# Two attention blocks and two feed-forward blocks on one core: the splitting of the score maxima may go to GpSimd, three release times are set anew, and the order is drawn again

## The chip, the cores and the metric

One core of a Trainium2 chip runs the whole program. The engines are TensorE (PE in the profile; its weight loads are PEld), VectorE (DVE), ScalarE (ACT), GpSimd (POOL) and SyncE (SP), which here only issues DMAs. Every engine works through its own list of instructions in a fixed order and waits at the head of it until what the instruction needs is ready. The metric is device time in microseconds. Before the change it was 1161.88 us, the median of 3 runs (1161.06 to 1162.78).

## The reference, cut to what matters

The input is 128 sequences of 64 tokens with 128 features, and a context of the same shape. Four residual blocks follow one another:

```python
x = x + L0_xattn(layernorm(x), ctx)   # 16 heads of 8, layer norms, gate, layer norm of the output
x = x + L0_ffn(layernorm(x))          # silu(w1 x) * (w2 x); two 512x512 layers with gelu; w3
x = x + L1_xattn(layernorm(x), ctx)   # 16 heads of 8, biases
x = x + L1_ffn(layernorm(x))          # relu(W1 x + b1), W2, b2

# inside either attention block
scores = einsum('bhqd,bhkd->bhqk', q, k) * 8 ** -0.5
attn = softmax(scores, axis=-1)
out = einsum('bhqk,bkhd->bqhd', attn, v) @ Wo + bo
```

The softmax subtracts the maximum of each row of scores. In the kernel this maximum is one per query, per group of heads, and it is taken off the scores by a matmul.

## The kernel before, in words

**Tiles.** The 8192 tokens are cut into 16 chunks of 512 tokens, 8 sequences each. For each chunk there are four stages: `attention0`, `ffn0`, `attention1` and `ffn1`. An attention stage has a part for the context (`context0` or `context1`: keys and values) and one for the queries, and then two halves (`attend`) of four sequences each.

**One half of an attention** (lines 614 to 712): 16 score matmuls write four PSUM banks (L629); VectorE takes the negated maxima over the keys out of PSUM, 128x32 numbers (L633, "max"); four small instructions split each of them into three bfloat16 numbers whose sum is the maximum (L642 to L645, "parts"); TensorE transposes these (L649, "max transpose"), ScalarE copies them out (L652), TensorE writes the scores again with the maxima taken off (L661, "scores less max"), ScalarE takes the exponential (L666), TensorE forms the weighted values and their sums (L680), ScalarE and VectorE sort these by masks (L690, L691, L693, L694), VectorE takes the reciprocal and shuffles it (L697, L698), and GpSimd multiplies (L712). Two such halves are followed by the product with the output weights (L740).

**The feed-forward block `ffn0`** has four gated pieces (L872 and L873 on TensorE, L876 on ScalarE, L878 and L879 on VectorE). Its two 512x512 layers are done with seven products of quarter matrices in place of eight (L928); for that GpSimd forms four differences of the activations for each layer (L910), and once, at the start, four sums of the weights for each layer (L865, in `weights`). These sums write tiles `ws` and `wh`. All products of a layer come after its weight sums.

**The order.** No engine's list is written out by hand. A planner in the kernel (`Order`) runs while the program is built. Each stage is a generator that yields operations (`Op`) with an engine or a choice of engines; `LENGTHS` gives the length of each operation on each engine, `RESOURCES` the number of buffers. At each step the planner takes, among all streams that could go on, the operation with the earliest start, and among equals the one with the lowest priority number plus a small random draw. The draws depend on `DRAWS`, one seed for each 50 us of the planner's clock; a seed of 0 means no draw. Where an operation names two engines, the planner takes the one on which it would end first (`start_of`). It also keeps GpSimd operations and those VectorE operations that are named in `PORT` ("z", "parts", "gate sums", "gained") from running at the same time in its plan. Whatever it assumes, on the chip each engine only follows its list and its semaphores.

**What is loaded when.** SyncE issues the loads of the start in one queue: context and tokens of chunk 0, `col`, the head mask, `wa0`, chunk 1, `row` (the vectors that are added along the features, on all partitions), `w12`, `wh` (2 MB), chunk 2, and four further weights. The planner knows of these by a list of made-up loads, `landed`, whose times it takes as given: a stream whose `ends` hold one of them isn't planned before that time. In the kernel before there are six; the weight sums of both layers are released by the last one, at 20.0.

**Two output biases.** `out_bias` (L436 to L444) multiplies the bias of the values by the output weights on TensorE (L440), and adds the output bias from `row` on VectorE (L443). The one for the first attention block is `early_bias`. It has no release time in the kernel before; its addition waits on the chip until `row` has landed.

**Fillers.** While its clock is below 95 (`RAMP`), the planner puts small matmuls on a blank tile (L405) where it expects TensorE to be idle.

Of the kernel before, what the change touches and what calls it, by code (L numbers as in the profile page):

```python
# [11 lines left out]
ALU = mybir.AluOpType  # L12
# [22 lines left out]
for _n, _w in _COLS:  # L35
# [17 lines left out]


STRETCH = 50.0
DRAWS = [121, 0, 0, 0, 0, 384, 0, 0, 0, 615, 0, 0, 0, 0, 0, 0, 0, 67, 0, 0, 564, 0, 762, 0]
SPREAD = 0.1
SWAP = [*range(16, 32), *range(16)]

# [2 lines left out]
PE, DVE, ACT, POOL, SP = "PE", "DVE", "ACT", "POOL", "SP"  # L62
# [9 lines left out]
        "product": (0.865, -0.2), "f1": (0.865, -0.2),  # L72
    },
    DVE: {
        "bias+": 0.28, "masks": 1.2, "gate weights": 0.4, "folds": 1.9, "moments": 1.07, "z": 1.05, "copied": 0.68,
        "scaled": 0.75, "qx": 1.5, "kx": 1.5, "vb": 1.8, "max": 2.3, "parts": 0.8, "reciprocal": 2.2, "o2": 0.83,
        "from bank": 0.68, "gate sums": 1.3, "gate": 0.4, "gained": 1.1, "gated": 1.45, "sum": 0.68, "saved": 0.68,
        "relu": 0.7,
# [3 lines left out]
        "two masked": 0.84, "gate exp": 0.25, "tanh": 0.69, "saved": 0.59, "gelu": 0.91, "relu": 0.69,  # L82
    },
    POOL: {
        "blank": 0.2, "blank values": 2.1, "rsqrt": 1.84, "rsqrt gate": 2.15, "oT": 0.73, "add": 1.27,
        "difference": 1.27, "weights": 1.27,
    },
    SP: {"load": (0.9, 4.0), "load again": (0.9, 4.0), "store": (0.5, 3.0)},
# [63 lines left out]
class Order:  # L152
# [63 lines left out]
    def draw(self):  # L216

        self.drawn += 1
        seed = DRAWS[min(int(self.clock[PE] / STRETCH), len(DRAWS) - 1)]
        x = (self.drawn * 2654435761 + seed * 2246822519) & 0xFFFFFFFF  # L220
# [83 lines left out]
def kernel(  # L304
# [16 lines left out]
    nc = tc.nc  # L321
# [13 lines left out]
    def tile_of(slot, shape, dtype=F32):  # L335

        kind, i = slot
        if kind != "bank":
            return work.tile(list(shape), dtype, tag=f"{kind}{i}", name=f"{kind}{i}")
        n = 1  # L340
        for d in shape[1:]:
            n *= d
        t = banks[:, i, :]
        t = t[:, 0:n] if dtype is F32 else t.bitcast(dtype)[:, 0:n]
        if len(shape) == 2:
            return t
        names = "abc"[: len(shape) - 1]
        return t.rearrange(
            "p (" + " ".join(names) + ") -> p " + " ".join(names), **dict(zip(names[1:], shape[2:]))
        )  # L350
# [49 lines left out]
    blank = const.tile([P, P], BF16, tag="blank", name="blank")  # L400
# [27 lines left out]
    def colv(name, k=0):  # L428
        s = COL[name]
        return col[:, s.start + k : s.start + k + 1]  # L430
# [5 lines left out]
    def out_bias(w, bv, bo, tag):  # L436

        pe = yield Op(PE, "bias", get={"bank": 1})
        ps = tile_of(pe.slots["bank"][0], (P, D))
        nc.tensor.matmul(ps, colv(bv).to_broadcast([P, P]), w, start=True, stop=True)  # L440
        yield Op(DVE, "bias+", put=pe.slots["bank"])
        t = const.tile([P, D], F32, tag=tag, name=tag)
        nc.vector.tensor_tensor(t, ps, row[:, ROW[bo], :], ALU.add)  # L443
        biases[tag] = t.unsqueeze(1).to_broadcast([P, NG, D])  # L444
# [36 lines left out]
    biases, masked, gates, folded, early_bias, late = {}, [], [], [], [], []  # L481
    made_weights, weights_of = {}, []
# [131 lines left out]
    def attend(got, half):  # L614
# [17 lines left out]
        m = small.tile([P, 4, 2 * HS], F32, tag="m", name="m")  # L632
# [4 lines left out]
            ALU.max,  # L637
            negate=True,
        )
        yield Op(DVE, "parts")  # L640
        part = [nm[:, :, 8 * j : 8 * j + 8] for j in range(3)]
        nc.vector.tensor_copy(part[0], m)  # L642
        nc.vector.tensor_tensor(m, m, part[0], ALU.subtract)
        nc.vector.tensor_copy(part[1], m)
        nc.vector.tensor_tensor(part[2], m, part[1], ALU.subtract)  # L645
        yield folded
        pe = yield Op(PE, "max transpose", get={"bank": 1, "nmT": 1}, put=mx.slots["nm"])
        pt = tile_of(pe.slots["bank"][0], (P, P), BF16)
# [1 line left out]
        op = yield Op(ACT, "max copied", put=pe.slots["bank"])  # L650
# [44 lines left out]
        op = yield Op(DVE, "reciprocal", get={"rec": 1}, put=pv.slots["su"])  # L695
# [6 lines left out]
        if "oT" not in got:  # L702
            given = got["oT given"] = Stream(None, 0, ())
            got["oT"] = None
            op = yield Op(POOL, "oT", get={"wk": 1}, put=done)
# [8 lines left out]
    def attention(got, prio):  # L714

        halves = []
        for half in range(2):
            halves.append((yield (attend(got, half), prio)))
        yield halves
        yield Op(NONE, "free", put=got["free"])  # L720
        return got["oT"].rearrange("p h s q -> p (h s q)"), got["oT_slots"]
# [97 lines left out]
    def attention0(ci, prio):  # L819
        got = {"free": []}  # L820
        xt = x_sb[ci]
        con = yield (context0(ci, got, prio), prio)
        if ci < 2:
            yield Op(NONE, "free", after=landed[3 * ci + 1])
        z, fz = yield from normalised(xt, twice=True)
        qnT, fq = yield from transposed(z, (), colv("L0_xattn_ln_q_g"), colv("L0_xattn_ln_q_b"))
        gat = yield (gate0(z, fz, got), prio)
        got["qx"], f = yield from queries(wa0[:, 0, :], qnT, bq0, fq)
        got["free"] += f
        yield [con]  # L830
        add = yield (biased0(xt), prio)
        oT, fo = yield from attention(got, prio)
        po, fp, fw = yield from token_major([(groups(oT), wa0[:, 3, :])], fo, own=True)
        yield early_bias
        yield Op(DVE, "from bank", put=fp)
        o = tile_of(fw[0], (P, NG, D))
        nc.vector.tensor_tensor(o, po, biases["bo0"], ALU.add)
        yield [gat]
        y, fy, rs = yield from normalised(
            o, gate=got["gate"], gain=row[:, ROW["L0_xattn_ln_o_g"], :]  # L840
        )
        yield [add]
        yield Op(DVE, "gained", put=fy + fw)
        for g in range(NG):
            nc.vector.scalar_tensor_tensor(  # L845
                xt[:, g, :], y[:, g, :], rs[:, g : g + 1], xt[:, g, :], ALU.mult, ALU.add
            )
# [4 lines left out]
    def weights(l):  # L852

        a = [[wh[:, l, 2 * j : 2 * j + 2, 256 * i : 256 * i + 256] for j in range(2)] for i in range(2)]
        s = [ws[:, l, n] for n in range(3)]
        for out, x, y, f in (
            (s[0], a[1][0], a[1][1], ALU.add),
            (s[1], s[0], a[0][0], ALU.subtract),  # L860
            (a[1][0], a[0][0], a[1][0], ALU.subtract),
            (s[2], a[0][1], s[1], ALU.subtract),
        ):
            yield Op(POOL, "weights")
            nc.gpsimd.tensor_tensor(out, x, y, f)  # L865

        made_weights[l] = [a[0][0], a[0][1], s[2], a[1][1], s[0], s[1], a[1][0]]
# [119 lines left out]
    def ffn0(ci, prio):  # L987
        xt = x_sb[ci]
        z, fz = yield from normalised(xt)
        zT, fz = yield from transposed(z, fz)  # L990
        fz = Last(fz, 4)
        b, made = {}, []
        yield from two_halves(b)
        for k in range(4):
            made.append((yield (gated(k, zT, fz, b), prio)))
        yield made[:1]
        h = [Both(made[0], made[1]), Both(made[2], made[3])]
        ready = [[h[0], h[0]], [h[1], h[1]]]
        for l in range(2):
            c = {}  # L1000
            ready = yield from square(l, b, ready, c, prio)
            b = c
            if l == 0:
                marks[ci].done = True
        yield ready[0] + ready[1]
        ps, fp, fw = yield from token_major(
            [
                (lambda g, k=k: b[k // 2][0][:, g // 2, k % 2, g % 2 * P : g % 2 * P + P], w3[:, k, :])
                for k in range(4)
            ],  # L1010
            b[0][1] + b[1][1],
            own=True,
        )
        yield Op(DVE, "from bank", put=fp)
        y = tile_of(fw[0], (P, NG, D))
        nc.vector.tensor_tensor(y, ps, rowv("L0_ffn_w3_s"), ALU.mult)
        yield Op(POOL, "add", put=fw)
        nc.gpsimd.tensor_tensor(xt, xt, y, ALU.add)
# [67 lines left out]
    order.add(loads(), 0)  # L1086
    a0, f0, a1, f1 = [], [], [], []

    landed = [Op(SP, "load") for _ in range(6)]
    for op, us in zip(landed, (0.0, 0.8, 2.2, 4.0, 5.0, 20.0)):  # L1090
        op.end, op.lag = us, 0.0
    early_vb, early_nm = order.take("vb", N_VB), order.take("nm", N_NM)
    order.add(blanks(), 1.2)
# [3 lines left out]
    folded.append(order.add(folds(), 1.6))  # L1097
    for l in range(2):
        weights_of.append(order.add(weights(l), 2.5 + l))
        weights_of[l].ends = [landed[5]]  # L1100
    early_bias.append(order.add(out_bias(wa0[:, 3, :], "L0_xattn_bv", "L0_xattn_bo", "bo0"), 1.5))
    for ci in range(NCH):
        marks.append(Stream(None, 0, ()))
        pa = 1 if ci else 0.5
        a0.append(order.add(attention0(ci, pa), pa, a0[-2:-1] + arrived[ci : ci + 1] + marks[-AHEAD - 1 : -AHEAD]))
        if ci == 0:
            late.append(order.add(out_bias(wa1[:, 3, :], "L1_xattn_b_v", "L1_xattn_b_o", "bo1"), 1.5, a0))
        first = ci == NCH - 1
        pf = -0.5 if first else 3 + ci / 100
        f0.append(order.add(ffn0(ci, pf), pf, [a0[ci]] + f0[-2:-1]))  # L1110
        a1.append(order.add(attention1(ci, 0), 0, [f0[ci]] + a1[-2:-1]))
        f1.append(order.add(ffn1(ci, 4), 4, [a1[ci]] + f1[-5:-4]))
# [52 lines left out]
```

## Time and profile before

The profiled execution took 1162.56 us; the span from its first to its last instruction is 1160.7 us, so 1.9 us lie around it. The mean granted TensorE clock was 0.989.

| engine | busy us | share of the span | instructions |
|---|---|---|---|
| PE | 1111.9 | 96% | 13758 |
| PEld | 867.8 | 75% | 13758 |
| DVE | 894.9 | 77% | 2239 |
| ACT | 724.6 | 62% | 1262 |
| POOL | 461.7 | 40% | 685 |

A row of the profile's list of groups names a line, an engine and an operation, what it writes and reads, the number of instructions, and after the bar their busy time and the mean of one. These are the rows that the change bears on:

| line, engine | what | count | busy us | mean ns |
|---|---|---|---|---|
| L633 DVE | maxima | 64 | 146.0 | 2282 |
| L642 DVE | parts, first copy | 64 | 16.6 | 260 |
| L643 DVE | parts, first difference | 64 | 16.6 | 260 |
| L644 DVE | parts, second copy | 64 | 16.0 | 249 |
| L645 DVE | parts, second difference | 64 | 14.3 | 224 |
| L865 POOL | weight sums | 8 | 10.3 | 1264 to 1294 |
| L443 DVE | output biases | 2 | 0.6 | 284 |
| L405 PE | fillers | 248 | 22.4 | 256 (pipelined) |

A wait is put down to what ended last before the waiting instruction could start. TensorE's busy time counts the fillers too, so it isn't all of use.

### The profile page before, as it was taken

How to read it: one execution, taken by the hardware profiler on the slowest of the kernel's cores; microseconds unless marked ns; L12 is line 12 of the kernel's file. 1: busy time of each engine (PE TensorE's matmuls, PEld its weight loads, DVE VectorE, ACT ScalarE, POOL GpSimd, SP SyncE). 2: the span in 40 equal slices, each digit the busy share in tenths (PEclk: the TensorE clock that was granted, in tenths of full speed). 3: DMA queues.
4: the chain of work that ended last, by engine and by line, in shares of the span. 5: the costliest groups of instructions: out<-in, count | busy, mean ns of one | idle time of the engine just before them, and what ended most of it. 6: DMA issues, size and time to landing. Idle time of an engine off the chain costs nothing. (4 is left out here: it accounts for less than half of the span.)

```text
span 1160.7 us, 32599 instructions
## 1 busy us (share of the span) xinstructions
PE 1111.9 (96%) x13758; PEld 867.8 (75%) x13758; DVE 894.9 (77%) x2239; ACT 724.6 (62%) x1262; POOL 461.7 (40%) x685
## 2 busy tenths in 40 slices
PE   7688999999999999999999999999999999999998
PEld 6557777876688767786788768876877788687776
DVE  6787798978768967888898877699587889647671
ACT  4365766676876657657667757575676656645643
POOL 7234343633523525424444325353336433434220
PEclk9799999999999999999999999999999999999999
DMA  7000100010000100000000010100010200000001
GB/s 251 2 11 1 28 2 20 11 29 1 20 11 3 38 11 19 11 29 11 2 2 3 2 37 2 38 2 2 2 37 1 65 2 3 11 10 1 2 30 37
DMA packets 35378, 23.21 MB, mean 20 GB/s; under 512 B 1440, under 2 KB 34208, under 8 KB 35104
## 3 DMA queue, kind: packets, MB, share of 16 engines
q1 hardware_dynamic: 35232, 21.13, 6.1%
q8 instruction: 108, 1.77, 0.6%
q14 instruction: 38, 0.31, 0.1%
HBM read 16.93 MB, written 4.19 MB: 18 GB/s over the span
## 5 line engine op out<-in xcount | busy, mean ns | idle before, releaser
L633 DVE TENSOR_REDUCE m<-banks 128x32 f32<-128x2048 f32 x64 | 146.0, 2282 | 17.9 <-PE banks L629 17.6
L712 POOL TENSOR_TENSOR wk<-av,rec 128x256 f32<-128x256 f32 x64 | 46.8, 731 | 280.8 <-DVE rec L698 207.9
L666 ACT ACTIVATE e<-banks 128x2048 f32<-128x2048 f32 x64 | 120.1, 1877 | 38.3 <-PE banks L661 36.4
L928 PE MATMUL banks<-wk,wh 128*128 128x256 f32 x512 | 127.1, 385 | 0.0
L928 PE MATMUL banks<-hd,wh 128*128 128x256 f32 x512 | 125.8, 384 | 0.8 <-ACT nmT L652 0.8
L928 PE MATMUL banks<-wk,ws 128*128 128x256 f32 x512 | 125.3, 385 | 0.0
L947 ACT ACTIVATE hd<-hd,col 128x256 f32<-128x256 f32 x192 | 85.4, 499 | 42.7 <-DVE hd L954 42.3
L697 DVE RECIPROCAL su<-su 128x256 f32<-128x256 f32 x64 | 111.5, 1742 | 0.0
L928 PEld LDWEIGHTS banks<-wk,ws 128*128 128x128 f32 x512 | 94.9, 192 | 18.4 <-issue 5.0
L928 PEld LDWEIGHTS banks<-hd,wh 128*128 128x128 f32 x512 | 93.2, 190 | 19.2 <-issue 3.8
L928 PEld LDWEIGHTS banks<-wk,wh 128*128 128x128 f32 x512 | 94.8, 191 | 15.3 <-issue 1.0
L954 DVE TENSOR_TENSOR hd<-banks,hd 128x512 f32<-128x512 f32 x96 | 65.2, 686 | 50.9 <-PE banks L928 35.0
L500 POOL TENSOR_TENSOR nr<-nv,neg_half 128x4 f32<-128x4 f32 x96 | 97.5, 1015 | 8.0
L486 ACT COPY hd<-banks 128x512 f32<-128x512 f32 x73 | 42.8, 586 | 85.5 <-PE banks L928 83.8
L910 POOL TENSOR_TENSOR wk<-hd,wk 128x512 f32<-128x512 f32 x64 | 81.7, 1278 | 36.1 <-DVE hd L879 17.5
L539 ACT ACTIVATE wk<-x,nb,nr 128x128 f32<-128x128 f32 x204 | 83.4, 484 | 14.5 <-POOL nb L530 13.5
L629 PEld LDWEIGHTS banks<-kx,qx 32*128 32x128 f32 x2048 | 63.8, 186 | 24.9 <-issue 7.6
L680 PEld LDWEIGHTS banks<-e,vblk 128*32 128x32 f32 x4096 | 60.2, 110 | 28.6 <-ACT e L666 12.1
L629 PE MATMUL banks<-kx,qx 32*128 32x128 f32 x2048 | 75.7, 283 | 5.1 <-DVE m L633 2.0
L680 PE MATMUL banks<-e,vblk 128*32 128x64 f32 x4096 | 70.4, 220 | 4.9 <-ACT e L666 4.7
L661 PE MATMUL banks<-qx,kx 32*128 32x128 f32 x2048 | 74.0, 284 | 0.0
L910 POOL TENSOR_TENSOR wk<-hd 128x512 f32<-128x512 f32 x32 | 40.9, 1279 | 79.9 <-ACT hd L947 36.1
(132 smaller groups left out, 2383.8 us busy)
## 6 DMA issues: line engine op xcount, KB each, us to landing
c<-in_c_dram SPq DMA_DIRECT2D x32, 256.0 KB, 3.1
x<-in_x_dram SPq DMA_DIRECT2D x16, 256.0 KB, 3.4
out_dram<-x SPq DMA_DIRECT2D x16, 256.0 KB, 2.3
wh<-in_w_h_dram SPq DMA_DIRECT2D x1, 2048.0 KB, 13.3
wa<-in_w_a_dram SPq DMA_DIRECT2D x2, 256.0 KB, 5.4
w<-in_w_dram SPq DMA_DIRECT2D x1, 512.0 KB, 7.3
wf<-in_w_f_dram SPq DMA_DIRECT2D x2, 256.0 KB, 7.0
row<-in_rows_dram SPq DMA_DIRECT2D x1, 384.0 KB, 6.6
```

Of the source, the lines that this page charges most:

```text
L500: nc.gpsimd.tensor_tensor(rs, ve, neg_half, ALU.pow)
L539: nc.scalar.activation(z[:, g, :], src[:, g, :], AF.Identity, bias=nb[:, g : g + 1], scale=rs[:, g : g + 1])
L629: nc.tensor.matmul(sc[:, g, s, :], qs[h, s, :], ks[h, s, :], start=True, stop=True)
L633: nc.vector.tensor_reduce(m, sc.rearrange("p g s (j k) -> p g (s j) k", j=2), AX.X, ALU.max, negate=True,)
L661: nc.tensor.matmul(sT[:, g, s, :], lhs, rhs, start=(n == 0 and s == 0), stop=(n == 1), skip_group_check=True)
L666: nc.scalar.activation(e.rearrange("p g s i q -> p (g s i q)"), sT.rearrange("p g s c -> p (g s c)"), AF.Exp, scale=SCALE,)
L680: nc.tensor.matmul(po[32 * g : 32 * g + 32, i, s, :], vb[:, 4 * (half * HS + s) + g, i : i + 2].rearrange("p h j d -> p (h j d)"), e[:, g, ...
L697: nc.vector.reciprocal(su, su)
L910: nc.gpsimd.tensor_tensor(T[n][0], x(), y(), ALU.subtract)
L928: nc.tensor.matmul(pieces[bank][0][:, o], w[:, k, o * P : (o + 1) * P], x[:, k], start=(new and k == 0 and o == 0), stop=(k == 1), skip_gr ...
L947: nc.scalar.activation(out(i, t)[:, o], (src or out(i, t))[:, o], AF.Gelu, scale=colv(scale, 2 * i + o))
L954: nc.vector.tensor_tensor(out(i, t), pieces[bank][0], out(i, t), ALU.add)
```

## The change: what it does

1. "parts" may be on VectorE or on GpSimd, by the planner's choice, half by half. Its length on GpSimd is set to 1.05; on VectorE it stays at 0.8.
2. The length of "z" on VectorE goes from 1.05 to 1.3.
3. The list `landed` has nine times in place of six. The weight sums of layer 0 are released at 24.0 and those of layer 1 at 40.0, in place of 20.0 for both. The first output bias is released at 7.2.
4. `DRAWS` has other seeds, so the planner draws another order.

```diff
-DRAWS = [121, 0, 0, 0, 0, 384, 0, 0, 0, 615, 0, 0, 0, 0, 0, 0, 0, 67, 0, 0, 564, 0, 762, 0]
+DRAWS = [583, 0, 0, 858, 0, 0, 0, 0, 2, 0, 0, 0, 0, 0, 0, 0, 0, 0, 174, 0, 0, 687, 994, 0]
...
-        "bias+": 0.28, "masks": 1.2, "gate weights": 0.4, "folds": 1.9, "moments": 1.07, "z": 1.05, "copied": 0.68,
+        "bias+": 0.28, "masks": 1.2, "gate weights": 0.4, "folds": 1.9, "moments": 1.07, "z": 1.3, "copied": 0.68,
...
-        "blank": 0.2, "blank values": 2.1, "rsqrt": 1.84, "rsqrt gate": 2.15, "oT": 0.73, "add": 1.27,
+        "blank": 0.2, "blank values": 2.1, "parts": 1.05, "rsqrt": 1.84, "rsqrt gate": 2.15, "oT": 0.73, "add": 1.27,
...
-        yield Op(DVE, "parts")
+        op = yield Op((DVE, POOL), "parts")
+        by = nc.gpsimd if op.engine == POOL else nc.vector
         part = [nm[:, :, 8 * j : 8 * j + 8] for j in range(3)]
-        nc.vector.tensor_copy(part[0], m)
-        nc.vector.tensor_tensor(m, m, part[0], ALU.subtract)
-        nc.vector.tensor_copy(part[1], m)
-        nc.vector.tensor_tensor(part[2], m, part[1], ALU.subtract)
+        by.tensor_copy(part[0], m)
+        by.tensor_tensor(m, m, part[0], ALU.subtract)
+        by.tensor_copy(part[1], m)
+        by.tensor_tensor(part[2], m, part[1], ALU.subtract)
...
-    landed = [Op(SP, "load") for _ in range(6)]
-    for op, us in zip(landed, (0.0, 0.8, 2.2, 4.0, 5.0, 20.0)):
+    landed = [Op(SP, "load") for _ in range(9)]
+    for op, us in zip(landed, (0.0, 0.8, 2.2, 4.0, 5.0, 7.2, 12.0, 24.0, 40.0)):
...
-        weights_of[l].ends = [landed[5]]
+        weights_of[l].ends = [landed[7 + l]]
     early_bias.append(order.add(out_bias(wa0[:, 3, :], "L0_xattn_bv", "L0_xattn_bo", "bo0"), 1.5))
+    early_bias[0].ends = [landed[5]]
```

The arithmetic is the same in both kernels. What the built lists show of the new order: of the 64 splittings of maxima 38 are on GpSimd and 26 on VectorE; there are 259 fillers in place of 248; ScalarE loads its tables 69 times in place of 67; some copies and maskings have changed between ScalarE and VectorE. SyncE's first sixteen loads are in the same order as before. At the start VectorE's list now has the moments of chunk 0, the gate weights, the masks, the folds, the moments of chunk 1's context, the scaling of chunk 0's query side, the moments of chunk 1's tokens, and only then the output bias. The list then holds the attention of the chunks 0, 1 and 2 to its end before the first gated piece of `ffn0`, and from there the `ffn0` of the chunks 0 and 1 side by side; in the kernel before the first gated piece of chunk 0 comes before the maxima of chunk 2 are transposed.

## The prediction

> **What bounds the kernel now.** I read the row of slices first, then busy time in three stretches, then what TensorE waits for in the first 100 us, then VectorE's timeline there.
>
> ```profile
> PE   7688999999999999999999999999999999999998
> DVE  6787798978768967888898877699587889647671
> PEclk9799999999999999999999999999999999999999
> ```
>
> Each digit is a fortieth of the span, 29 us. TensorE is full from the fifth slice to the end; only the start has holes. The next view gives busy us of PE, PEld, DVE, ACT and POOL, then granted clock, DMA share and GB/s.
>
> ```profile
> 0.00:50.00 50.00, 33.76 (x551) 29.19 (x551) 32.24 (x107) 20.37 (x38) 27.65 (x49) 0.90 0.45 146
> 50.00:100.00 50.00, 40.23 (x548) 30.32 (x552) 41.69 (x120) 21.92 (x39) 17.87 (x33) 0.90 0.02 7
> 100.00:1160.00 1060.00, 1037.88 (x12675) 808.33 (x12663) 820.94 (x2014) 682.30 (x1185) 416.15 (x603) 1.00 0.05 15
> ```
>
> TensorE idles 16.2 + 9.8 = 26.0 us before 100 us, and 22.1 in the other 1060, some 4 of them at the end. Of its busy time before 100 us some 22 are fillers (L405, no use). So about 48 of the first 100 us are not work; later there are only 18 us to win. Who holds it up at the start, by total wait:
>
> ```profile
> PE banks L649 <- DVE nmax L642: 4.1, 1, 4.1
> PE banks L760 <- DVE gw L757: 4.0, 1, 4.0
> PE banks L553 <- DVE m L633: 3.5, 2, 1.9
> PE banks L740 <- DVE m L633: 3.4, 1, 3.4
> ```
>
> VectorE ends every one of them. Its own timeline (start, duration, then idle before and releaser) shows two faults:
>
> ```profile
> 5.70 0.36 DVE L514 BATCH_NORM_AGGREGATE mv<-st 128x2 f32<-128x6 f32 x4
> 10.99 0.29 DVE L443 TENSOR_TENSOR bo<-banks,row 128x128 f32<-128x128 f32 x1 [4.93 <-DMA row<-in_rows_dram]
> ...
> 27.05 1.35 DVE L805 SCALAR_TENSOR_TENSOR wk<-wk,gw 128x128 f32<-128x128 f32 x1
> ...
> 31.99 0.18 DVE L642 CAST nmax<-m 128x32 bf16<-128x32 f32 x1
> 32.21 1.20 DVE L643 TENSOR_TENSOR m<-m,nmax 128x32 f32<-128x32 f32 x1
> 33.44 0.18 DVE L644 CAST nmax<-m 128x32 bf16<-128x32 f32 x1
> ```
>
> First, the output bias waits 4.93 us for `row`, with masks, gate weights and folds queued behind it. Second, beside GpSimd's back-to-back adds (L865 and L817, 23.1 to 33.4) a gate sum takes 1.35 us where it takes 0.28 later, and L643 1.20 instead of 0.19.
>
> **The bias (part 3) and the order of the start.** I walk the new list with these durations. TensorE: 60 fillers end at 6.9, 19 more at 0.062 (28 took 1.73) at 8.1, the gate product 0.75 at 8.85. VectorE does moments and masks meanwhile, then the gate copy 0.26 and folds 1.84: 10.95. The same block ends at 14.50 before: a lead of 3.5. `row` landed at 10.9 before (issued 4.27, 6.6 to landing), and the bias now comes at about 14, behind moments and scaling, so its wait goes; SP's queue up to `row` is unmoved. What is late next is ScalarE's scaling of the two inputs and TensorE's fixed list: first scores at 17.6 (21.8 before).
>
> The first maximum then starts at 20.45 (one of four gate sums still meets an add), and the second follows at once, ending at 24.9; before, four slowed gate sums lay between and it ended at 31.9. Lead 7.0. Here comes a loss: the second half's splitting is on VectorE, and from 24.0 GpSimd has the first weight sum, an add of chunk 1 and three more sums back to back. If each of the four small instructions meets one, as L643 did, they take 4 times 1.2 and end at 29.4 (lead 5.1 on 34.5); if not, at 25.9. I take the first, by the gate sums, of which three in a row did so. Then scaling 0.8, query product 0.9, the second scores 2.5: first exponential at 34.0 (38.6 before), last reciprocal of chunk 0 at 44.6 (49.2 before): lead 4.6.
>
> From there to the `ffn0` part VectorE has 34.5 us of work by the rows (four maxima 9.1, two reciprocals with shuffles 4.3, five moments of 1.1 to 1.2, the rest small) and waits: for GpSimd's last weight sums at the two "gained" groups, for ScalarE's normalised inputs, for chunk 2's exponentials. I get the first gated piece at 87.5. TensorE has then done 37.6 us of work: three attention chunks of 12.0 (transposes 0.9, k, q and v 2.7, scores 2.1, transposed maxima 0.2, second scores 2.9, weighted values 2.2, output 0.9; chunk 2 without output), biases and two transposes. So 49.9 us are not work. Before, the same sum at 99.6 gives 46.0 of work and 53.6 lost. **Lead 3.7**; without the collision 7.2. After it two `ffn0` run side by side, six gated pieces of 1.73 on TensorE against 1.45 on VectorE, so no new hole is due.
>
> **Weight sums (part 3).** Eight adds of about 1.28, 10.3 us in all, no more and no fewer; L865 started at 23.1 before, so 24.0 moves layer 0 little. Behind them in GpSimd's queue stand chunk 0's products (L712), splittings, and square roots. The products need these weights only near 90 us. Cost: the collisions counted above, nothing else.
>
> **Splitting (part 1).** 38 halves of 64 move. VectorE loses 38 x (260 + 260 + 249 + 224) = 37.7 us; with the copies and maskings moved between it and ScalarE (kx -16, qx +6, copies and scalings +28 instructions) it has about 31 us less, 864 in all; ScalarE has 4 less. GpSimd has no such row. Its nearest are 128x256 at 731, 128x512 at 1278 and 128x4 at about 200: 2.14 ns an element gives 0.25 for 128x32, at least 0.20. Four are 0.8 to 1.0, plus 0.08 between dependent ones (L499 at 5.20 for 0.19, L500 at 5.48) and 0.14 for the handover: I take 1.4, range 1.2 to 1.5, against 0.86 for VectorE's chain undisturbed and 1.1 on average. A half's maxima arrive 0.3 to 0.5 later. After 100 us TensorE's order has other chunks' work between scores and transposed maxima; idle there was 1.9 us in 3 waits for L645. Where that cover is gone, a late half costs its lateness. I take zero for TensorE after 100 us: VectorE's relief and the handover bear on the same 18 us of holes.
>
> **A rule that speaks against it.** The Trainium skill, "Perfetto Trace Analysis", section "Optimizing Scalar/DVE Operations", says that GpSimd and VectorE share an SBUF port, so shifting work between the two may gain nothing. The row shows the lock: L643 has a median of 192 ns, a mean of 260 and a maximum of 1269; means over medians (82, 68, 67, 32 ns) make 15.9 us of lock in 64 halves. By the rule, 38 x 1.0 us of port time only change hands and VectorE gains nothing. By the rows it is freed of 37.7 us, 9.5 of them lock (38/64 of 15.9), and the new GpSimd pieces can hold it 0.25 us each at most, 38 us if all 152 did, which they can't: most of VectorE's time is PSUM maxima, reciprocals and reads of banks. I take the rows. Neither shows on TensorE directly.
>
> **"z" and the draws.** The length changes no instruction; its rows say 4 x 450 ns on VectorE, and the list has four instructions fewer there. Two more table loads are 2.6 us on ScalarE (62% busy), hidden by its idle time. The draws move all the rest. Bound: all 18 us of holes gone, or as many new ones. I take zero. The end of TensorE's list has more than 10 us of other work between the last output product and the last normalised tile, and the closing L1049 and L740 groups as before: zero.
>
> **Sum.** Span 1160.7 - 3.7 = 1157.0; with the 1.9 around it 1158.9; the median of the runs shown lies 0.7 under the profiled 1162.56: **1158 us**.
>
> **Rivals.**
> *The relief also closes holes later.* For it: VectorE ends the most waits of TensorE after 100 us (about 10 of 18 us). Against: such holes come from order as well. Half of 18 closed and the start 2 us better: 1162 - 3.7 - 2 - 5 = 1151.
> *The lead is given back.* In-order lists meet later at the same draining of three chunks; collisions at "gained" cost more than I count. No change: 1162.
> *Slower: GpSimd's queue becomes the late one.* Its place is L642 to L645 behind square roots (L500, 1.02) or differences (L910, 1.28). For it: 38 new entries with a strict order, and a transposed maximum that comes late stops TensorE's whole list. Against: GpSimd is 40% busy (43% after). If 13 of 38 come 1.28 late uncovered, 16.6 us: 1162 - 3.7 + 16.6 = 1175. It decides from four late halves on (5.1 against 3.7).
> *It doesn't do what it says*: ruled out, the built list has 38 on GpSimd.
>
> **Chances.** Forecast 0.46, its own range 1152 to 1163; holes closed 0.14; given back 0.14; slower 0.26. A measurement tells about 0.2%, 2.3 us, from no change: 1159.6 to 1164.2 is "the same". Faster: 0.39 of the forecast and 0.14: 0.53. Same: 0.07, 0.10 of "given back" and 0.02: 0.19. Slower: the rest, 0.28. The range: 1149 (just beyond the second case) to 1170 (half of the slow case's way).
>
> **What would show it.** Right: L443 without a wait for `row`; second maximum ending near 25 us, first gated piece at 85 to 90; fewer than 26 us of TensorE idle before 100; splitting on GpSimd at about 0.25 an instruction; near 18 us idle later. Wrong: many waits of L649 for GpSimd's splitting, parts of 2 us, a "gained" or gate sum held at 1.3 each time, or new holes after 100 us for ScalarE's or VectorE's late results.

## The result, and the profile after

The changed kernel takes 1155.59 us (median of 4 runs, 1152.72 to 1156.21) against 1162.1 us before (4 runs): a ratio of 0.994, 95% interval 0.9921 to 0.9958. The forecast was 1158, faster. In the profiled executions the span falls from 1160.7 to 1154.0 us, by 6.7.

The row of slices of the changed kernel:

```profile
PE   7679999989999999999999999999999999999998
DVE  8788678859787867888757787788787688643762
PEclk9989999989999999999999999999999999999999
```

Again TensorE's holes are in the first slices; after them only the ninth (231 to 260 us) has an 8. The windows of the changed kernel (busy us of PE, PEld, DVE, ACT and POOL, granted clock, DMA share, GB/s), where the second stretch is longer than what is left of the span:

```profile
0.00:100.00 100.00, 73.90 (x1255) 58.08 (x1256) 82.97 (x232) 44.40 (x78) 45.83 (x93) 0.93 0.23 77
100.00:1200.00 1100.00, 1036.29 (x12516) 806.64 (x12514) 783.77 (x1869) 675.40 (x1173) 448.98 (x744) 1.00 0.05 14
```

In the first 100 us TensorE idles 26.1 us, as before (26.0). After them it idles 1054.0 - 1036.3 = 17.7 us; before it was 1060.7 - 1037.9 = 22.8. So by idle time alone the gain lies after 100 us. But 100 us is a mark on the clock, not in the work: by the sum of the prediction, TensorE has done 37.6 us of work when the first gated piece starts at 89.0, so 51.4 us are lost there; before, 53.6 were lost at 99.6. That is 2.2 us won at the start and about 4.5 later. The split is an estimate. TensorE's busy time without the fillers, 51.4 us of 99.6 before and 41.5 of 89.0 after, would make it 0.7 at the start; with the work done at a granted clock of 0.5 counted at half, about 3.

What ends TensorE's waits in the first 100 us of the changed kernel:

```profile
PE banks L650 <- DVE nmax L646: 7.0, 2, 5.3
PE banks L681 <- ACT e L667: 4.3, 6, 1.1
PE banks L577 <- DVE wk L562: 3.3, 3, 1.5
```

The 4.0 us for the gate weights are gone. VectorE's splittings (L646) still lead, and 5.3 of their 7.0 us come at the first transposed maximum of chunk 2. VectorE's timeline at the start of the changed kernel:

```profile
14.51 0.26 DVE L443 TENSOR_TENSOR bo<-banks,row 128x128 f32<-128x128 f32 x1
...
20.59 4.48 DVE L633 TENSOR_REDUCE m<-banks 128x32 f32<-128x2048 f32 x2
25.17 0.18 DVE L643 CAST nmax<-m 128x32 bf16<-128x32 f32 x1
25.39 1.18 DVE L644 TENSOR_TENSOR m<-m,nmax 128x32 f32<-128x32 f32 x1
26.60 1.18 DVE L645 CAST nmax<-m 128x32 bf16<-128x32 f32 x1
27.81 1.20 DVE L646 TENSOR_TENSOR nmax<-m,nmax 128x32 bf16<-128x32 f32 x1
```

The bias no longer waits for its vectors. The two maxima run together and end at 25.07 (31.9 before). Then come three small instructions of about 1.2 us each where 0.2 would do. Beside them GpSimd works through its adds:

```profile
25.25 1.26 POOL L818 TENSOR_TENSOR x<-x,row 128x512 f32<-128x512 f32 x1
26.48 1.26 POOL L866 TENSOR_TENSOR ws<-ws,wh 128x512 f32<-128x512 f32 x1
27.70 1.26 POOL L866 TENSOR_TENSOR wh<-wh 128x512 f32<-128x512 f32 x1
```

The three small instructions end at 26.56, 27.78 and 29.01, each 0.05 us after one of these adds. The splitting on GpSimd, among the groups of the changed kernel:

```profile
L644 POOL TENSOR_TENSOR m<-m,nmax 128x32 f32<-128x32 f32 x38 | 9.3, 245 | 3.1
L643 POOL CAST nmax<-m 128x32 bf16<-128x32 f32 x38 | 8.0, 211 | 98.8 <-DVE m L633 98.8
```

A difference takes 245 ns and a copy 211. The 98.8 us are idle time in which GpSimd stood at the head of a splitting and waited for VectorE's maxima.

### The profile page after: what moved, and what is told of

It reads as the page before. It is cut to its first block, busy times and chain, and to the rows that moved or that the text cites. A ratio compares the mean times of both kernels' runs of the same rounds, so it can differ in the third digit from the quotient of the medians.

```text
span 1154.0 us, 32569 instructions
## 1 busy us (share of the span) xinstructions
PE 1110.2 (96%) x13769; PEld 864.7 (75%) x13769; DVE 866.7 (75%) x2100; ACT 719.8 (62%) x1251; POOL 494.8 (43%) x837
## 5 line engine op out<-in xcount | busy, mean ns | idle before, releaser
L539 ACT ACTIVATE wk<-x,nb,nr 128x128 f32<-128x128 f32 x204 | 83.7, 484 | 27.4 <-POOL nb L530 27.2
L911 POOL TENSOR_TENSOR wk<-hd,wk 128x512 f32<-128x512 f32 x64 | 81.6, 1275 | 41.7 <-DVE hd L880 19.9
L486 ACT COPY hd<-banks 128x512 f32<-128x512 f32 x62 | 36.2, 584 | 77.3 <-PE banks L929 76.4
L873 PE MATMUL banks<-wk,w 128*128 128x512 f32 x128 | 66.8, 604 | 0.5 <-ACT nmT L653 0.4
## 6 DMA issues: line engine op xcount, KB each, us to landing
wh<-in_w_h_dram SPq DMA_DIRECT2D x1, 2048.0 KB, 13.2
```

The lines of the kernel that those rows point to most:

```text
L539: nc.scalar.activation(z[:, g, :], src[:, g, :], AF.Identity, bias=nb[:, g : g + 1], scale=rs[:, g : g + 1])
L873: nc.tensor.matmul(pa, w12[:, 0, k * P : (k + 1) * P], zT, start=True, stop=True)
L911: nc.gpsimd.tensor_tensor(T[n][0], x(), y(), ALU.subtract)
```

## The experiments

Any change to what the planner sees redraws the whole order. Most experiments therefore leave the plan alone and change only which engine an instruction is issued on, or where in VectorE's list it stands; TensorE's list is then the same, instruction for instruction. Each was timed next to the kernel before, on the same chip. All times are medians, and ratios are against the kernel before. "Old list" means the order of the kernel before, "its list" that of the changed kernel. What the new length of "z" and each of the release times do by themselves was not tried in the new list.

| run | us | ratio (95% interval) |
|---|---|---|
| changed kernel again | 1155.69 | 0.9957 (0.9944 to 0.997) |
| its list, 38 splittings back on VectorE | 1169.06 | 1.0066 (1.0053 to 1.0078) |
| its list, second half of chunk 0 on GpSimd too | 1148.92 | 0.9902 (0.9887 to 0.9917) |
| its list, all 64 splittings on GpSimd | 1147.93 | 0.9898 (0.9881 to 0.9915) |
| old list, late bias | 1156.99 | 0.9963 (0.9951 to 0.9976) |
| old list, all 64 splittings on GpSimd | 1148.27 | 0.9886 (0.987 to 0.9901) |
| the same, with a small load on VectorE | 1150.23 | 0.9907 (0.9891 to 0.9922) |
| the same, with the full load | 1148.38 | 0.9905 (0.9888 to 0.9922) |
| the same without load, but VectorE's place kept | 1150.63 | 0.9914 (0.99 to 0.9927) |
| old list, all on GpSimd and late bias | 1142.89 | 0.9842 (0.9827 to 0.9856) |
| changed kernel, old draws | 1174.06 | 1.0113 (1.0099 to 1.0128) |
| kernel before, new draws | 1182.94 | 1.0198 (1.0181 to 1.0214) |

**1. The 38 splittings put back.** In the changed kernel:

```diff
-        by = nc.gpsimd if op.engine == POOL else nc.vector
+        by = nc.vector
```

> The list of the changed kernel on every engine, but the 38 splittings that it has on GpSimd are issued on VectorE at the same places. If VectorE's relief closed the later holes (theory Relief): about 1160 to 1162 us, TensorE idle after 100 us back at 18 to 22 us. If the new order alone closed them (theory Order): 1155 to 1157, idle after 100 us at most 15 us. If splitting on GpSimd costs by its latency (theory Queue): below 1154.

Measured: 1169.06 us, 13.5 more than the changed kernel and 8 more than the kernel before. It is beyond what any of the three theories had said, in the direction of Relief. So this list without the splitting on GpSimd is slower than the old one, and in it the relief is worth more than the whole gain. (The list was drawn for splittings on GpSimd. What the planner would have drawn without them was not tried.) The first gated piece came only 0.8 us later, the last transposed maximum 13.2 us later. The second window of this run, from 100 us on:

```profile
100.00:1200.00 1100.00, 1038.17 (x12520) 806.03 (x12518) 815.34 (x2011) 676.68 (x1173) 417.71 (x604) 1.00 0.05 14
```

TensorE idles 1067.2 - 1038.2 = 29.0 us after 100 us in place of 17.7. Theory Order falls. Matmul by matmul, the two traces are still level at 440 us, and all 13 us are lost behind that. There TensorE's transposed maxima wait 5.8 us for VectorE's splittings, where the changed kernel has no such wait:

```profile
PE banks L650 <- DVE nmax L646: 5.8, 5, 1.6
```

**2. The old list with all splittings on GpSimd.** In the kernel before:

```diff
-        nc.vector.tensor_copy(part[0], m)
-        nc.vector.tensor_tensor(m, m, part[0], ALU.subtract)
-        nc.vector.tensor_copy(part[1], m)
-        nc.vector.tensor_tensor(part[2], m, part[1], ALU.subtract)
+        nc.gpsimd.tensor_copy(part[0], m)
+        nc.gpsimd.tensor_tensor(m, m, part[0], ALU.subtract)
+        nc.gpsimd.tensor_copy(part[1], m)
+        nc.gpsimd.tensor_tensor(part[2], m, part[1], ALU.subtract)
```

> The list of the kernel before on every engine, but all 64 splittings are issued on GpSimd at the same places. Relief: 1156 to 1159 us, TensorE idle after 100 us below 15 us. Order: 1161 to 1163, idle there 18 to 22 us. Queue (splittings stuck behind square roots and differences, with a place that was not planned for them): above 1165, with waits of the transposed maxima for GpSimd's last splitting.

Measured: 1148.27 us, 13.0 less than before and 7 less than the changed kernel, with a list that was never planned for it. Compared at the same instructions of TensorE in the two traces, 4.9 us are won by the first gated piece, 9.3 by the fifth (at 114.2 us in the kernel before), and 13.1 at the end. That is more than Relief had said, but in another place: TensorE still idles 18.6 us after 100 us, and the start gains more. The feared queue of GpSimd doesn't show. The timeline of the kernel before, VectorE and then GpSimd, just after its first gated pieces (start, duration, engine, line, operation, tiles; in brackets the idle time before it and what ended that):

```profile
89.44 1.13 DVE L644 CAST nmax<-m 128x32 bf16<-128x32 f32 x1
90.60 1.20 DVE L645 TENSOR_TENSOR nmax<-m,nmax 128x32 bf16<-128x32 f32 x1
91.72 1.29 DVE L642 CAST nmax<-m 128x32 bf16<-128x32 f32 x1
```

```profile
89.23 1.30 POOL L910 TENSOR_TENSOR wk<-hd,wk 128x512 f32<-128x512 f32 x1 [1.63 <-DVE nmax L642]
90.49 1.26 POOL L910 TENSOR_TENSOR wk<-hd,hd 128x512 f32<-128x512 f32 x1
91.71 1.26 POOL L910 TENSOR_TENSOR wk<-hd,wk 128x512 f32<-128x512 f32 x1
```

The three small VectorE instructions that take over 1 us end at 90.57, 91.80 and 93.01, each about 0.05 us after one of GpSimd's (90.53, 91.75, 92.97): three instructions of 0.2 us take 3.6. Both transposed maxima of chunk 2 wait for them, and behind them TensorE's own work is slow for a while:

```profile
91.85 0.23 PE L649 MATMUL banks<-identb,nmax 128*128 128x128 bf16 x1 [1.54 <-DVE nmax L645]
93.73 0.23 PE L649 MATMUL banks<-identb,nmax 128*128 128x128 bf16 x1 [1.54 <-DVE nmax L645]
95.48 3.33 PE L928 MATMUL banks<-wk,ws 128*128 128x256 f32 x8
```

The window over that stretch shows a granted clock of 0.50, and below it stand the same eight matmuls in experiment 2, where the stretch has the full clock:

```profile
94.80:98.20 3.40, 3.40 (x22) 2.64 (x19) 0.00 (x0) 1.88 (x1) 1.61 (x4) 0.50 0.00 0
```

```profile
87.53 1.99 PE L928 MATMUL banks<-wk,ws 128*128 128x256 f32 x8
```

The two waits (3.1 us) and this stretch (1.3 us in the eight matmuls alone) make most of the 4.4 us between the first and the fifth gated piece. Whether the slow stretch came of the waits was not tested. The clock also spreads the runs of one kernel: those of experiment 2 go from 1145.20 us at a mean granted clock of 0.995 to 1150.32 at 0.989, so 2 us between two kernels say little.

So is it VectorE's time that counts, or its waits? Experiments 3 and 4 ask.

**3. A load in place of the splitting.** Experiment 2, and after each splitting on GpSimd four reductions of a constant on VectorE that nobody waits for:

```diff
+        for j in range(4):
+            nc.vector.tensor_reduce(idle[:, j : j + 1], ident[:, 0:32], AX.X, ALU.max)
```

> The kernel before with all 64 splittings on GpSimd, and in their place on VectorE four small reductions of a constant (128x32 to 128x1), that nobody waits for and that load VectorE about as long as undisturbed splittings. If VectorE's time was what counted (theory Time): most of the 13 us come back, 1157 to 1161. If it was the splittings' waits for the port and the place of the maxima in VectorE's list (theory Lock): at most 1152.

Measured: 1150.23 us, some 2 of the 13 us given back (ratio 0.9907 against 0.9886, with intervals that overlap). VectorE's busy time rose by only 23.5 us (857.0 against 833.5), less than the expectation had meant, so the load was made larger: `ident[:, 0:P]`.

> As the run with four small reductions in place of the splittings, but each over 128 numbers, so that they take about 0.8 us a half, as four undisturbed splittings do (the smaller ones took 0.4). If VectorE's time counts (theory Time): the 1.9 us that the smaller load gave back grow to most of the 13, at least 1156. If waits for the port and the holding up of what is behind a waiting splitting count (theory Lock): twice the smaller load's price, 1150 to 1153.

Measured: 1148.38 us, ratio 0.9905, with 50 us more on VectorE than experiment 2 (883.9 against 833.5), most of what the splitting had cost (894.9 before). Twice the load gives back no more than the small one, and whether it is 2 us or nothing the intervals can't tell. The group of the load in this run shows why it is harmless (nanoseconds least, median and most):

```profile
L648 DVE TENSOR_REDUCE idle<-ident x256: 250/276/282, 28.4 to 1100.4; 128x1 f32<-128x128 f32 x128
```

None of these reductions took more than 282 ns. The four instructions of the splitting in the kernel before have longest ones of 1207 to 1291 ns. Theory Time falls: the load gives back about 2 us at most by the medians, not most of the 13. (The Trainium skill, "SBUF — State Buffer", section "Who interferes with whom", says that a reduction never contends for the port; these rows agree.)

**4. The place in VectorE's list.** A splitting on GpSimd also starts earlier: on average 1.26 us after the end of its maximum, against 2.03 before, because it need not wait for VectorE's list to come to it. So in experiment 2 the place was put back: GpSimd splits a copy of the maxima that VectorE makes, by a reduction over one element (189 ns at most), where the splitting had stood.

```diff
+        m_max, m = m, copies[len(taken) % 4]
+        taken.append(m)
+        nc.vector.tensor_reduce(
+            m.rearrange("p g s -> p (g s)"), m_max.rearrange("p g s -> p (g s)").unsqueeze(2), AX.X, ALU.max
+        )
```

> The kernel before with all 64 splittings on GpSimd, but each waits for one copy of the maxima that VectorE makes by a reduction at the place where its list had the splitting. So GpSimd cannot start a splitting earlier than VectorE's list came to it. If the place in VectorE's list was what cost (theory Place): most of the 13 us come back, at least 1157. If it was the small VectorE instructions' waits for the port and what they held up (theory Port): 1148 to 1152.

Measured: 1150.63 us. The splitting now starts 2.18 us after its maximum and ends 3.32 after it, later than before (3.12), and 10.0 us are still won (1160.61 for the kernel before beside it). The place is thus worth some 3 us at most (ratios 0.9914 and 0.9886), and VectorE's time about 2 by experiment 3. What is left, 8 to 10 of the 13 us, is by exclusion the waits of the splittings for the port they share with GpSimd, and what these hold up.

**5. The bias alone.** In the kernel before, the addition is held back and issued after the next five VectorE operations:

```diff
-        nc.vector.tensor_tensor(t, ps, row[:, ROW[bo], :], ALU.add)
+        add = lambda: nc.vector.tensor_tensor(t, ps, row[:, ROW[bo], :], ALU.add)
+        if tag == "bo0":
+            order.held = (pe.slots["bank"][0], add)
+        else:
+            add()
```

> The list of the kernel before, but the addition of the first output bias comes after the scaling of chunk 0's query side on VectorE in place of before the masks. If the wait for the row vectors is worth what the start showed (theory Bias): masks and folds done near 9.5 us in place of 14.5, first exponentials 2 to 4 us earlier, 1158 to 1160 us. If GpSimd's adds and the gate sums take it back (theory Given back): 1161 to 1163.

Measured: 1156.99 us, 4.3 less (ratio 0.9963), a little more than expected. The first transposed maximum is 3.8 us earlier, the first gated piece 3.9, and so it stays until 800 us. Masks and folds were done at 10.8, not 9.5: the last folds met GpSimd's memset, of which more below.

**6. The collision with the weight sums.** The changed kernel, with one splitting more on GpSimd, ahead of the sums:

```diff
-        by = nc.gpsimd if op.engine == POOL else nc.vector
+        splits.append(op); by = nc.gpsimd if op.engine == POOL or len(splits) == 2 else nc.vector
```

> The changed kernel, but the splitting of the second half of chunk 0 goes to GpSimd, ahead of the weight sums that it met on VectorE. If the collision at 25 to 29 us is on the path (theory Collision): the first gated piece 2 to 3.5 us earlier than 89.0, 1152 to 1153.5 us. If the next late thing (scaling, exponentials) hides it: 1155 to 1156.

Measured: 1148.92 us (4 of 5 runs within 0.4 us of it, one at 1153.64), 6.7 less than the changed kernel, more than expected. GpSimd's timeline of this run:

```profile
22.83 0.21 POOL L643 CAST nmax<-m 128x32 bf16<-128x32 f32 x1 [1.06 <-DVE m L633]
...
23.72 0.33 POOL L646 TENSOR_TENSOR nmax<-m,nmax 128x32 bf16<-128x32 f32 x1
24.02 1.31 POOL L866 TENSOR_TENSOR ws<-wh 128x512 f32<-128x512 f32 x1
```

The splitting is done at 24.05 in place of 29.01, ahead of the weight sums. The first exponential starts at 27.2 in place of 33.9, and the first gated piece at 83.2 in place of 89.0. Not all of that is the edit's: in this profile the first maximum started at 18.28 against 20.59, before the edit bears on anything (last section). That leaves 4.4 of the 6.7 us at the first exponential to the edit; what the other 2.3 hang on is open.

**7. All 64 on GpSimd in the new list.**

> The list of the changed kernel on every engine, but all 64 splittings on GpSimd. If each half moved is worth what the 38 were worth (13.5 / 38 = 0.36 us a half, theory Each): 1155.6 - 26 x 0.36 = 1146. If only those at the start still counted (theory Start): 1149, as the run with the second half moved. If GpSimd's queue is full where the list had not planned for it (Queue): above 1152.

Measured: 1147.93 us (1147.58 to 1152.78), as theory Start said: against experiment 6 the other 25 halves are worth about 1 us, which the spread of the runs can't tell from nothing. A half that is moved has no fixed price.

**8. Both gains in the old list.** Experiments 2 and 5 together:

> The kernel before with all 64 splittings on GpSimd and the late output bias. If the two gains add up: 1161.3 - 13.0 - 4.3 = 1144. If they hide one another at the start: 1147 to 1149.

Measured: 1142.89 us, 18.2 less than before; 13.0 and 4.3 would make 17.3. They add up. It is the fastest version found, 13 us below the changed kernel, with the old draws and no new plan.

**9. The draws.** Only the line `DRAWS` is exchanged:

> The changed kernel with the draws of the kernel before; the planner makes another order. If the draws are a matter of a few us either way (theory Lottery): anywhere from 1148 to 1166. If the change's gain doesn't hang on them: 1152 to 1158.

> The kernel before with the draws of the changed one, nothing else. Lottery: 1155 to 1175, most likely slower, since these seeds were not made for this kernel. If the new draws were what helped: 1155 to 1158.

Measured: 1174.06 and 1182.94 us, 18 and 23 us more than each kernel with its own seeds, beyond both ranges. As far as these two runs show, a list of seeds is good for its own plan only.

**10. The changed kernel once more.**

> The changed kernel itself, beside the others on their chip: 1153 to 1156.5 us. If the one vector instruction that met GpSimd's memset at 10 us is a matter of chance (theory Chance), its runs fall into two groups some 2 to 3 us apart; if not, they lie within 1 us.

Measured: five runs within 1155.18 to 1156.09 and one at 1160.02, with a granted clock of 0.985 against 0.988 to 0.991 in the others. These are not the two groups that theory Chance had in mind.

## Why the prediction was right, and where it was not

**The bias and the walk through the start** held step by step. The times in us:

| step | predicted | measured |
|---|---|---|
| second maximum ends | 24.9 | 25.07 |
| its splitting ends, with the collision | 29.4 | 29.01 |
| first exponential starts | 34.0 | 33.9 |
| last reciprocal of chunk 0, with its shuffle, ends | 44.6 | 44.2 |
| first gated piece starts | 87.5 | 89.0 |

The lead was to be 3.7 and is 2.2 by the same sum. The last step took 44.8 us for 42.9; TensorE's longest wait in it is the 5.3 us for the splitting of chunk 2's first maximum. The bias alone is worth 3.9 at the first gated piece of the old list (experiment 5).

**Weight sums.** "Cost: the collisions counted above, nothing else" fits the runs, though the release times were not tried by themselves; one splitting moved out of their way won 4.4 us at the first exponential (3.5 were counted).

**Splitting: "I take zero for TensorE after 100 us" failed.** The length on GpSimd was right: 0.21 to 0.245 us an instruction for 0.25, and 1.25 from the end of the maximum to the end of the splitting, on average over the 38, for 1.4. VectorE's relief was in the right direction. Read strictly, the rule that the prediction weighs against its rows would have left VectorE without any gain. Between experiment 1 and the changed kernel, whose lists are the same, VectorE's busy time falls by 895.4 - 866.7 = 28.7 us. But 37.7 were counted, with 9.5 of lock, and the lock that fell away is only 9.1 - 5.1 = 4.0 us (means over the medians of the kernel before).

The wrong part is that none of it was let through to TensorE. In the lists of these runs it came through: 13.5 us in the new one, 13.0 in the old one. For the old list experiments 3 and 4 show by which road: the freed time counts for about 2 us, the place for 3 at most, and the waits for the port for the rest. The prediction counted these waits as VectorE's time alone; but they stand at the head of a list in which maxima, reciprocals and gated pieces are queued, and TensorE's fixed list stops for those.

For the new list no such experiment was made, but the trace of experiment 1 shows a large part of the same road. From 440 us on, where all is lost, its 39 splittings on VectorE lie 7.7 us above the medians, the 15 of the changed kernel 1.1. Of the five waits of TensorE for a splitting there, the longest, 1.6 us, ends with this one, whose last two instructions end at 1025.04 and 1026.28, just behind two of GpSimd's differences (L911), which end at 1025.00 and 1026.23:

```profile
1023.91 1.13 DVE L645 CAST nmax<-m 128x32 bf16<-128x32 f32 x1
1025.08 1.20 DVE L646 TENSOR_TENSOR nmax<-m,nmax 128x32 bf16<-128x32 f32 x1
```

Another, of 1.5 us, is mostly place: there the splitting stands behind two instructions of a gated piece in VectorE's list. How the 13.5 us divide between port, place and time in this list stays open.

**Draws: "I take zero", with a bound of 18 us either way.** The bound was too narrow (18 and 23 us with exchanged seeds), and zero was wrong for this draw: the new list with all splittings on VectorE is 7.8 us slower than the old one, although it still has some 1.4 us of the lead at its first gated piece (2.2 less 0.8). So with the splittings on VectorE what was drawn behind the start loses about 9 us, and the splitting on GpSimd wins 13.5. The loss is no constant of the order: with the late bias in both lists, the new one is 12.1 us slower with all splittings on VectorE (1169.06 against 1156.99) and 5.0 slower with all on GpSimd (1147.93 against 1142.89).

**The number was luck in part.** Two terms set to zero, of opposite signs, left about 4.5 us, and with the lead of 2.2 the forecast came out 2.4 us from the measured time. The start was understood; that so little remained of the rest was not foreseen. The rival "holes closed" (1151) had the right direction after 100 us. Its sum does not fit its words, though: half of 18 us is 9, not 5, and with 9 it would be 1147. **The clock** has no term in the prediction at all. By the mean granted clock of the two profiles, 0.989 and 0.991, it can have a share of at most some 2 us in the 6.7 between their spans (an estimate: 1.1% of 1160.7 less 0.9% of 1154.0).

**The slower rival** had GpSimd's queue late from four halves on. In the changed kernel TensorE's transposing matmuls (L650) wait 7.1 us, 7.0 of them for splittings on VectorE; their weight loads wait 0.4 us, in two waits, for splittings on GpSimd. Even 64 splittings on GpSimd made neither list slower.

## What to carry to other kernels

An instruction that takes 0.2 us and waits 1.2 for a port is no small instruction: look at its mean against its median and at its longest, and at what stands behind it in its list. A dummy load of equal length tells whether an engine's time or its waits hold the kernel up, and a change of engine that leaves every list's order alone tells what a part of a change is worth when a planner would redraw everything. Before a new plan is searched, the small edit should be tried in the old one: here it was 7 us better, and 13 with the late bias.

## What was not expected of the hardware

VectorE's wait for GpSimd is not only a matter of adds. A copy or a scaling in SBUF also waits for a memset. Timelines of the changed kernel and, after it, of the run with the second half on GpSimd:

```profile
9.95 1.63 DVE L784 TENSOR_SCALAR half_s<-col 128x4 f32<-128x4 f32 x1
...
10.17 1.38 POOL L470 MEMSET vblk<- 128x1536 f32 x1
```

```profile
9.46 0.16 DVE L784 TENSOR_SCALAR half_s<-col 128x4 f32<-128x4 f32 x1
...
9.97 1.38 POOL L470 MEMSET vblk<- 128x1536 f32 x1
```

The lists are the same up to here. In one execution the scaling of 128x4 numbers was done before the memset began and took 0.16 us; in the other it took 1.63 and ended at 11.58, the memset at 11.55. In the second profile of the changed kernel the casts just before it took 2.02 us in place of 0.63. Half a microsecond more or less of VectorE's start thus makes 2 us behind the scaling. The two profiles in the new list with more splittings on GpSimd (experiments 6 and 7) are in the early case, both profiles of the changed kernel and that of experiment 1 in the late one; why was not settled. The opposite is as clear: reductions on VectorE, of SBUF or of PSUM, never waited: in the run with the full load 282 ns at most of 256, and of the 64 maxima 2294 at most with a median of 2282.
